# Moving one line of a hand-ordered kernel: WKV's transposes, a down product's place, and scales read as broadcasts

## The chip, the cores and the metric

The kernel runs on one core of one Trainium2 chip. The metric is the device time of one execution in microseconds (us). TensorE is called PE in the profile, VectorE DVE, ScalarE ACT, GpSimd POOL, SyncE SP; PEld is TensorE's loading of weights.

## The reference, cut to what matters

Four elements of 512 rows by 512 columns go through four residual steps each:

```python
x = x + tanh(g_xattn[0]) * wkv(w, u, layernorm(x), ctx)            # a scan over the rows
x = x + tanh(g_ffn[0])   * bitlinear_ffn(layernorm(x), w1, w2, w3)  # 512 -> 2048 -> 512
x = x + tanh(g_xattn[1]) * int8_attention(layernorm(x), ctx, ...)   # 16 heads
x = x + tanh(g_ffn[1])   * ternary_linear(x, gamma, W)              # 512 -> 512
```

WKV is a recurrence for each column with a running maximum. At each row it gives y = (A p + E v) / (A q + E); p, q and the maximum are carried on. The feed-forward quantises its inputs and hidden values in groups of 64 and has weights of one bit with one scale. The attention quantises rows and the weights of its query and output projections to 8 bits. The last step has ternary weights.

## The kernel before

An element's x stays in SBUF as four tiles of 128 rows. The four elements are staggered: while one is in its feed-forward, the element after it does WKV and the one before it does attention or the last step. The layers are generators, and each `yield` ends a step.

**The order of the work** is written by hand. A `line` is a generator with the places at which its steps come; `run` always takes the step with the smallest place. From the second element on, the unit of place is one element's feed-forward, divided into `SLOTS` = 17 parts. In this document a *place* is one such part: one unit of the feed-forward (one tile of rows by one quarter of the 2048 hidden columns). TensorE's instructions are pinned to this order, since the first of a step stands behind the last of the step before (`in_turn`, `next_turn`). Those of the other engines are placed by a scheduler that follows the dependencies and the program's order. Each engine then executes its instructions in order.

**The feed-forward** (`ffn_layer`) gives each unit four steps, at .0, .25, .5 and .75 of its place: the first up product with tanh (`gate`), the down product of the unit two back (`down`), the second up product with the gating and the quantising (`gated`), and the transposes of the unit before (`gate_parts`, tile tp_ps). The quantised hidden row goes through DVE (L736, maxima L231, reciprocal, product L666), ACT (L670) and POOL (L671). It is transposed, and is then split by ACT (L682) and DVE (L683) into the two parts of hr that the down product reads (ff_acc). The first element has its weights `made` beside it, in a first stage of its own that lasts to about 350 us.

**WKV** (`wkv_layer`) normalises and transposes the four row tiles (tiles wk_xn, one buffer; wk_ps; copy L573) and then treats four chunks of 128 columns. `in_steps(chains, 8)` starts a chunk every eight steps. A chunk's steps are: the maximum's scan (L588) and POOL's difference; two steps of relus and exponentials on ACT (L601, L603); the scan for q and the product with A; the scan for p (L623); the reciprocals (L629, two of 128x256); the product y (L634); the transposes of y (tile wy_ps) and the update of x (L640). A step is a quarter of a place, so a chunk takes two places. For elements 2 and 3 each chunk's v is loaded by a DMA of SP's queue into the one buffer that wk_xn also uses.

**The attention** of the element before has four steps a place, at .95, .20, .45 and .70: scores of one pair (s_ps, maximum L929, exponential L931), the values' product (o_ps) and transposes of the exponentials (pt_ps, copied by ACT L951), scores of the other pair, and again transposes and the collection of the output (ot_ps, at_o on DVE L989). Scores and up products share three PSUM banks (hp). All transposes, o_ps, ot_ps and query products share three others (m), so a transpose waits until the tile three before it in its ring has been read. In the first stage m has two banks.

**Scales.** Each row tile of attention is quantised with one scale a row. To have it along the columns, POOL fills a 128x128 tile with it (at_full, L848), and TensorE transposes that tile (sx_ps). Once, `output_scales` does the same for the output weights' scales: four copies on DVE (w_full, L429), four transposes (pb_ps), and one product (L431).

```python
def transpose(*args):
    return in_turn(nc.tensor.transpose(*args))
```

A transpose loads its input as weights and multiplies by the identity.

Of the kernel before, what the change touches and what calls it, by code (L numbers as in the profile page):

```python
# [10 lines left out]
F32 = mybir.dt.float32  # L11
# [5 lines left out]
ALU = mybir.AluOpType  # L17
# [4 lines left out]
P = 128  # L22
# [8 lines left out]
def kernel(  # L31
# [138 lines left out]
    def transpose(*args):  # L170
        return in_turn(nc.tensor.transpose(*args))  # L171
# [119 lines left out]
    class Weights:  # L291
# [132 lines left out]
        def output_scales(self):  # L424

            pb = bank("pb_ps")
            for j in range(NC):
                full = self.pool.tile([P, P], F32, name="w_full", tag="w_full", bufs=2)
                nc.vector.tensor_copy(full, self.sp[:, j : j + 1].to_broadcast([P, P]))  # L429
                transpose(pb[:, j * P : (j + 1) * P], full, ident)  # L430
            nc.vector.tensor_scalar(swp_b, pb, gates[:, 1:2], None, ALU.mult)  # L431
            nc.sync.dma_start(out=bp_b, in_=bcast(bp))
            nc.vector.tensor_scalar(bp_b, bp_b, gates[:, 1:2], None, ALU.mult)
# [117 lines left out]
    def wkv_layer(b, xb):  # L551

        kT = wk.tile([P, NC, T], F32, name=f"wk_k{b}", tag="wk_k")
        if b:
            r = layernorm(xb, pinned=True)
            yield  # L560
        else:
            r = layernorm(xb)
        for t in range(NT):
            if b or t == 0:
                xn = wk.tile([P, D], F32, name="wk_xn", tag="wk_v")
            else:
                xn = ff.tile([P, D], F32, name="wk_xn", tag="ff_a", bufs=3)
            centred(xn, xb, r, t)
            yield
            pt = bank("wk_ps")  # L570
            for c in range(NC):
                transpose(pt[:, c * P : (c + 1) * P], xn[:, c * P : (c + 1) * P], ident)
            nc.scalar.copy(kT[:, :, t * P : (t + 1) * P], blocks(pt))  # L573

        def chunk(c):
            def row(name):
                if b == 0 and c % 3:
                    return ff.tile([P, T + 1], F32, name=name, tag=(None, "ff_a", "xp")[c % 3], bufs=3)
                return wk.tile([P, T + 1], F32, name=name, tag=name)

            if b > 1:
                v = wk.tile([P, T], F32, name="wk_v", tag="wk_v")
                nc.sync.dma_start(out=v, in_=cD[b][:, c, :])
            k = kT[:, c, :]
            w_c, u_c, w_n, u_n = (a[:, c : c + 1] for a in (wc, uc, wcn, ucn))
            o = row("wk_o")
            nc.gpsimd.memset(o[:, 0:1], NEG_INF)
            nc.vector.tensor_tensor_scan(  # L588
                o[:, 1:], w_c.to_broadcast([P, T]), k, NEG_INF, ALU.add, ALU.max
            )  # L590

            if b == 0 and c < 3:
                e = ring.tile([P, 4, T], F32, name="wk_e", tag="w")
            else:
                e = wk.tile([P, 4, T], F32, name="wk_e", tag="wk_e")
            z = row("wk_p")[:, 0:T]
            nc.gpsimd.tensor_tensor(z, k, o[:, 0:T], ALU.subtract)
            if b:
                yield True
            for i, (sign, at) in enumerate(((1.0, u_c), (-1.0, w_c), (-1.0, u_n), (1.0, w_n))):  # L600
                nc.scalar.activation(e[:, i, :], z, AF.Relu, bias=at, scale=sign)  # L601
                if b and i % 2:
                    nc.scalar.activation(  # L603
                        e[:, i - 1 : i + 1, :], e[:, i - 1 : i + 1, :], AF.Exp, scale=-1.0
                    )
                    yield True
            if b == 0:
                exps[c] = nc.scalar.activation(e, e, AF.Exp, scale=-1.0)
                yield True

            A, E2, E, A2 = (e[:, i, :] for i in range(4))
            if b < 2:
                v = context.cT[b][:, c, :]
            q = row("wk_q")
            p = row("wk_p")
            nc.gpsimd.memset(q[:, 0:1], 0.0)
            nc.gpsimd.memset(p[:, 0:1], 0.0)  # L617
            nc.vector.tensor_tensor_scan(q[:, 1:], A2, E2, 0.0, ALU.mult, ALU.add)  # L618
            nc.gpsimd.tensor_tensor(E2, E2, v, ALU.mult)
            den = q[:, 0:T]  # L620
            nc.vector.tensor_tensor(den, A, den, ALU.mult)
            yield True
            nc.vector.tensor_tensor_scan(p[:, 1:], A2, E2, 0.0, ALU.mult, ALU.add)  # L623
            nc.gpsimd.tensor_tensor(den, den, E, ALU.add)
            nc.gpsimd.tensor_tensor(E, E, v, ALU.mult)
            yield True
            for h in range(2):
                half = den[:, h * (T // 2) : (h + 1) * (T // 2)]
                nc.vector.reciprocal(half, half)  # L629
            nc.gpsimd.tensor_tensor(A, A, p[:, 0:T], ALU.mult)  # L630
            nc.gpsimd.tensor_tensor(A, A, E, ALU.add)
            yield True
            y = E2
            nc.vector.tensor_tensor(y, A, den, ALU.mult)  # L634
            yield True
            pt = bank("wy_ps")
            for t in range(NT):
                transpose(pt[:, t * P : (t + 1) * P], y[:, t * P : (t + 1) * P], ident)
            xc = xb[:, :, c * P : (c + 1) * P]
            nc.vector.scalar_tensor_tensor(xc, blocks(pt), gates[:, 0:1], xc, ALU.mult, ALU.add)  # L640
            yield True

        chains = [chunk(c) for c in range(NC)]
        if b:
            yield from in_steps(chains, 8)
            return

        for chain in chains:
            next(chain)
            yield  # L650
        yield from in_steps(chains, (0, 1, 2, 4))
# [36 lines left out]
    def ffn_layer(xb, made=None):  # L688
# [88 lines left out]
            weights(1, 0)  # L777


        for n in range(len(units) + 2):  # L780
            now = n < len(units)
            if now:
                t, f = units[n]
                i = t % size


                if i == min(1, size - 1) and not made:
                    weights(2, f)
                after = units[n + 1] if n + 1 < len(units) else None
                if after and after[1] != f and not made:  # L790
                    weights(0, after[1])
                z = gate(up(t, f, 0))
            yield
            if n > 1:
                down(*units[n - 2])
            yield
            if size == NT and n + 1 < NT:
                inputs_parts(n + 1)
                next_turn()
            if now:  # L800
                gated(t, f, z, up(t, f, 1))
            if now and after and after[1] != f and not made:
                weights(1, after[1])
            yield
            if 0 < n <= len(units):
                gate_parts(*units[n - 1])

            if now and size < NT:
                next_turn()
                if (t, f) in ((0, 1), (1, 2)):  # L810
                    inputs(f + 1)
                elif (t, f) in ((1, 1), (1, 3)):
                    inputs_parts(2 if f == 1 else 3)
            if n < len(units) + 1:
                yield
# [4 lines left out]
    def attention_layer(b, xb, pool, tiles=range(NT)):  # L820
# [18 lines left out]
        def prepared(t, r):  # L839
            xn = row("at_xn")  # L840
            centred_aside(xn, xb, r, t)
            s = sm.tile([P, 2], F32, name="at_s", tag="at_s")
            yield True
            absmax(s[:, 0:1], xn)
            int8_scale(s[:, 0:1], s[:, 1:2], s[:, 0:1])
            rounded(xn, s[:, 1:2])
            full = row("at_full")[:, 0:P]
            nc.gpsimd.tensor_scalar(full, ones, s[:, 0:1], None, ALU.mult)  # L848
            yield True
            transposed_rows(xqT[:, :, t * P : (t + 1) * P], xn)  # L850
            sp = bank("sx_ps")[:, 0:P]
            transpose(sp, full, ident)
            nc.scalar.copy(sxb[:, t * P : (t + 1) * P], sp)

            nc.gpsimd.tensor_tensor(xb[:, t, :], xb[:, t, :], bp_b, ALU.add)
            yield True
# [312 lines left out]
    with (  # L1169
# [105 lines left out]
        for b in (2, 3):  # L1275
            line(
                next_batch(b),
                (b - 1.0 - 4.2 / SLOTS, b - 1.0 - 4.2 / SLOTS, 1),
                (b - 1.0 - 3.2 / SLOTS, b - 1.0 - 3.2 / SLOTS, 1),
                (b - 1.0 + 1.8 / SLOTS, b - 1.0 + 5.8 / SLOTS, 4),  # L1280
                (b - 1.0 + 5.05 / SLOTS, b - 1.0 + 13.05 / SLOTS, 32),
            )
        run(0.99)
    nc.sync.dma_start(out=gamma_b, in_=bcast(gamma))
# [75 lines left out]
```

## Time and profile before

| what | value |
|---|---|
| time, median of 3 runs | 1141.91 us (1141.67 to 1142.8) |
| the profiled execution's own time | 1140.58 us |
| its span | 1138.8 us |
| mean granted TensorE clock | 0.948 |
| PE busy | 967.2 us (85%), 5520 instructions |
| DVE busy | 877.1 us (77%), 1889 |
| ACT busy | 722.0 us (63%), 1482 |
| POOL busy | 320.4 us (28%), 317 |

The profile is of one execution. A row of the timeline has a start, a duration, the engine, the line, the operation, output<-inputs and, in brackets, how long the engine had been idle before it and what ended that. Where an instruction waits for several others, the one that came last is named. Rows can merge neighbours (x2, x8). A row of the table by stretch has, for each engine, the busy time and the number of instructions, and then the granted clock, the DMA engines' share and their rate.

### The profile page before, as it was taken

What the parts mean: (1) busy time and instruction counts of PE and PEld (TensorE: products, weight loads), DVE (VectorE), ACT (ScalarE), POOL (GpSimd) and SP (SyncE); (2) the same over time, 40 slices, a digit from 0 to 9 for tenths busy, and PEclk for the clock granted to TensorE, in tenths of its full rate; (3) what the DMA queues carried; (4) which work ended last, traced back from release to release, by engine and by line L of the source; (5) the groups of instructions that cost most, each with busy time, mean ns of one, the idle gap of its engine ahead of it and who ended that gap; (6) DMA issues with size and microseconds to landing.
All of it is one profiled execution on the core that took longest, in us unless ns stands there. A gap on an engine that the chain in (4) does not pass through costs nothing.

```text
span 1138.8 us, 16572 instructions
## 1 busy us (share of the span) xinstructions
PE 967.2 (85%) x5520; PEld 679.9 (60%) x5548; DVE 877.1 (77%) x1889; ACT 722.0 (63%) x1482; POOL 320.4 (28%) x317
## 2 busy tenths in 40 slices
PE   4887898888877968889998897999999899888983
PEld 3344565555555756666776565777777677555651
DVE  5965547679878788999769899977689756688766
ACT  5777555454214576757777677687676577877763
POOL 3821014341305244441124535412122410112000
PEclk8898999999889989999998999999999999998997
DMA  8197745364425545654645544565474572333400
GB/s 277 47 299 281 282 163 184 116 236 148 148 76 192 209 166 177 186 164 169 226 173 185 169 162 137 174 217 163 176 234 149 181 232 76 105 109 103 126 5 37
DMA packets 85668, 189.58 MB, mean 166 GB/s; under 512 B 12240, under 2 KB 36816, under 8 KB 74576
## 3 DMA queue, kind: packets, MB, share of 16 engines
q1 hardware_dynamic: 85584, 188.53, 49.4%
q8 instruction: 44, 0.72, 0.3%
q14 instruction: 40, 0.33, 0.1%
HBM read 148.65 MB, written 39.85 MB: 166 GB/s over the span
## 4 chain that ended last, share of the span: by engine, by line
PE 47%; DVE 27%; ACT 15%; issue 4%; POOL 4%; DMA 2%; SPq 0%; ACTq 0%; POOLq 0%; DVEq 0%
PE ff_hp L168 13%; PE ff_acc L168 7%; PE pt_ps L171 6%; PE o_ps L168 4%; PE s_ps L168 3%; PE v_ps L168 3%; ACT at_P L931 3%; DVE at_nm L929 3%; DVE wk_q L629 3%; DVE qg_i L666 2%; PE qr_ps L171 2%; ACT wk_e L601 2%; PE tp_ps L171 2%; DVE wk_q L618 2%; ACT at_PT L951 2%
## 5 line engine op out<-in xcount | busy, mean ns | idle before, releaser
L168 PE MATMUL ff_hp<-wT,xp 128*128 128x512 f32 x1024 | 275.8, 413 | 5.9 <-ACT at_P L931 2.1
L168 PEld LDWEIGHTS ff_hp<-wT,xp 128*128 128x128 f32 x1024 | 197.0, 196 | 56.4 <-ACT at_P L931 4.6
L931 ACT ACTIVATE at_P<-s_ps,at_nm 128x512 f32<-128x512 f32 x256 | 174.6, 689 | 72.3 <-DVE at_nm L929 71.0
L929 DVE TENSOR_REDUCE at_nm<-s_ps 128x1 f32<-128x512 f32 x256 | 165.8, 678 | 28.5 <-PE s_ps L168 28.3
L671 POOL TENSOR_TENSOR ff_z<-qg_b,qg_s 128x512 f32<-128x512 bf16 x64 | 72.5, 1132 | 335.3 <-ACT qg_b L670 293.0
L951 ACT COPY at_PT<-pt_ps 128x512 f32<-128x512 f32 x224 | 124.0, 596 | 38.5 <-PE pt_ps L171 38.0
L171 PE MATMUL pt_ps<-ident,at_P 128*128 128x128 f32 x1024 | 140.9, 279 | 8.0 <-ACT at_PT L951 2.6
L168 PE MATMUL ff_acc<-wT,hr 128*128 128x512 f32 x512 | 137.9, 411 | 6.1 <-ACT hr L682 3.4
L171 PEld LDWEIGHTS pt_ps<-ident,at_P 128*128 128x128 f32 x1024 | 113.8, 141 | 48.9 <-issue 14.1
L168 PEld LDWEIGHTS ff_acc<-wT,hr 128*128 128x128 f32 x512 | 93.5, 192 | 27.0 <-ACT hr L682 4.3
L168 PE MATMUL s_ps<-at_kR,at_qR 128*128 128x512 f32 x256 | 97.6, 452 | 13.2 <-ACT at_P L931 5.4
L670 ACT CAST qg_b<-qg_i 128x512 bf16<-128x512 int8 x80 | 49.3, 617 | 59.8 <-DVE qg_i L666 53.8
L168 PE MATMUL o_ps<-at_PT,at_V 128*32 128x256 f32 x1024 | 73.0, 399 | 1.8 <-ACT at_PT L951 1.2
L731 ACT ACTIVATE ff_z<-ff_hp,coef 128x512 f32<-128x512 f32 x64 | 43.8, 684 | 46.4 <-PE ff_hp L168 42.9
L736 DVE SCALAR_TENSOR_TENSOR ff_z<-ff_hp,coef,ff_z 128x512 f32<-128x512 f32 x64 | 47.5, 743 | 29.4 <-PE ff_hp L168 29.1
L732 DVE SCALAR_TENSOR_TENSOR ff_z<-ff_z,ff_hp 128x512 f32<-128x512 f32 x64 | 43.6, 681 | 32.7 <-ACT ff_z L731 32.3
L168 PE MATMUL v_ps<-wkvT,cT 128*128 128x512 f32 x128 | 63.2, 642 | 4.2 <-ACT wT L316 3.2
L168 PE MATMUL k_ps<-cT,wkvT 128*128 128x512 f32 x128 | 61.1, 626 | 2.3 <-ACT wk_k L573 1.0
L168 PEld LDWEIGHTS s_ps<-at_kR,at_qR 128*128 128x128 f32 x256 | 45.5, 196 | 28.3 <-ACT at_P L931 13.1
L682 ACT CAST hr<-tp_ps 128x512 fp32r<-128x512 f32 x64 | 37.6, 587 | 35.6 <-PE tp_ps L171 35.6
L629 DVE RECIPROCAL wk_q<-wk_q 128x256 f32<-128x256 f32 x32 | 54.3, 1719 | 1.4 <-POOL wk_p L617 1.4
L171 PE MATMUL tp_ps<-ident,ff_z 128*128 128x128 f32 x256 | 39.9, 279 | 18.1 <-ACT at_PT L951 7.7
(179 smaller groups left out, 1757.3 us busy)
## 6 DMA issues: line engine op xcount, KB each, us to landing
wT<-wD SPq DMA_DIRECT2D x72, 1024.0 KB, 5.2
wn<-in_L_ffn_w_dram SPq DMA_DIRECT2D x18, 1024.0 KB, 6.2
at_kR<-kD SPq DMA_DIRECT2D x128, 128.0 KB, 2.9
at_qR<-qD SPq DMA_DIRECT2D x256, 64.0 KB, 2.2
wD<-wT SPq DMA_DIRECT2D x12, 1024.0 KB, 4.5
kD<-k_half SPq DMA_DIRECT2D x16, 512.0 KB, 3.2
qD<-at_half SPq DMA_DIRECT2D x32, 256.0 KB, 2.0
cn<-in_ctx_dram SPq DMA_DIRECT2D x8, 512.0 KB, 6.2
```

Source lines behind the costliest of these rows:

```text
L168: return in_turn(nc.tensor.matmul(*args, **kwargs))
L171: return in_turn(nc.tensor.transpose(*args))
L629: nc.vector.reciprocal(half, half)
L670: nc.scalar.copy(qb, qi)
L671: nc.gpsimd.tensor_tensor(grouped(src), grouped(qb), s.unsqueeze(2).to_broadcast([P, NG, GS]), ALU.mult)
L682: nc.scalar.copy(part[:, 0, :], pt)
L731: nc.scalar.activation(z, hp, AF.Tanh, scale=coef[:, 0:1])
L732: nc.vector.scalar_tensor_tensor(z, z, 1.0, hp, ALU.add, ALU.mult)
L736: nc.vector.scalar_tensor_tensor(z, hp, coef[:, 1:2], z, ALU.mult, ALU.mult)
L929: nc.vector.tensor_reduce(nm, sp, AX.X, ALU.max, negate=True)
L931: nc.scalar.activation(lanes[k, i, t], sp, AF.Exp, bias=nm, accum_out=sums[k][:, t, i : i + 1],)
L951: made[k] = nc.scalar.copy(dst, blocks(pt))
```

## The change

Four things. (1) In WKV for elements 1 to 3 an empty step stands between y and its transposes, so these come two steps after y; they now share a step with the beginning of the next chunk, which goes first in the program. The line of elements 2 and 3 has its 32 steps at 4.40 to 12.40 places instead of 5.05 to 13.05 (0.65 sooner), and its four normalising steps begin at 1.40 instead of 1.80. A chunk needs one more step, and the last transposes fall on the line's end. (2) In the first element's feed-forward the down product comes after the second up product, not before it. (3) The output scales are transposed from the column, repeated by a broadcast, without a copy. (4) So are the attention's row scales, without POOL's fill; the row buffer that it took is free for others.

```diff
             for j in range(NC):
-                full = self.pool.tile([P, P], F32, name="w_full", tag="w_full", bufs=2)
-                nc.vector.tensor_copy(full, self.sp[:, j : j + 1].to_broadcast([P, P]))
-                transpose(pb[:, j * P : (j + 1) * P], full, ident)
+                transpose(
+                    pb[:, j * P : (j + 1) * P],
+                    self.sp[:, j : j + 1].to_broadcast([P, P]),
+                    ident,
+                )
...
             nc.vector.tensor_tensor(y, A, den, ALU.mult)
             yield True
+            if b:
+                yield True
             pt = bank("wy_ps")
...
             yield
-            if n > 1:
-                down(*units[n - 2])
-            yield
+            if not made:
+                if n > 1:
+                    down(*units[n - 2])
+                yield
...
+            if made:
+                yield
+                if n > 1:
+                    down(*units[n - 2])
             yield
             if 0 < n <= len(units):
                 gate_parts(*units[n - 1])
...
-            full = row("at_full")[:, 0:P]
-            nc.gpsimd.tensor_scalar(full, ones, s[:, 0:1], None, ALU.mult)
             yield True
             transposed_rows(xqT[:, :, t * P : (t + 1) * P], xn)
             sp = bank("sx_ps")[:, 0:P]
-            transpose(sp, full, ident)
+            transpose(sp, s[:, 0:1].to_broadcast([P, P]), ident)
...
-                (b - 1.0 + 1.8 / SLOTS, b - 1.0 + 5.8 / SLOTS, 4),
-                (b - 1.0 + 5.05 / SLOTS, b - 1.0 + 13.05 / SLOTS, 32),
+                (b - 1.0 + 1.40 / SLOTS, b - 1.0 + 5.40 / SLOTS, 4),
+                (b - 1.0 + 4.40 / SLOTS, b - 1.0 + 12.40 / SLOTS, 32),
```

## The prediction

> **What bounds the kernel now.** I read the page's busy shares first, then its chain, then the table by stretch, then the timeline around the edited lines.
>
> ```profile
> PE 967.2 (85%) x5520; PEld 679.9 (60%) x5548; DVE 877.1 (77%) x1889; ACT 722.0 (63%) x1482; POOL 320.4 (28%) x317
> ...
> PE 47%; DVE 27%; ACT 15%; issue 4%; POOL 4%; DMA 2%; SPq 0%; ACTq 0%; POOLq 0%; DVEq 0%
> ```
>
> No engine is full over the span, and the chain goes back and forth between PE and DVE. So the stages matter. From one WKV transpose group to the next, in the stage where element 2's WKV runs (three of its four chunks):
>
> ```profile
> core 0: us, PE busy (x) PEld busy (x) DVE busy (x) ACT busy (x) POOL busy (x), PEclk, DMA share, GB/s
> 417.80:445.90 28.10, 24.55 (x144) 18.89 (x145) 23.33 (x37) 18.72 (x39) 10.92 (x12) 0.90 0.50 164
> 445.90:473.10 27.20, 24.24 (x143) 17.85 (x144) 25.22 (x40) 18.82 (x39) 11.36 (x12) 0.94 0.49 168
> 473.10:499.30 26.20, 22.12 (x141) 16.63 (x141) 25.44 (x50) 17.94 (x39) 13.55 (x14) 0.99 0.57 177
> ```
>
> A chunk's period is two places of the order, 27.2 us on average. DVE works 24.7 of it (97% in the last row), PE 22 to 24.5. Inside one period:
>
> ```profile
> 467.29 3.33 DVE L629 RECIPROCAL wk_q<-wk_q 128x256 f32<-128x256 f32 x2
> ...
> 469.90 0.63 PE L171 MATMUL tp_ps<-ident,ff_z 128*128 128x128 f32 x4
> ...
> 470.55 1.21 DVE L929 TENSOR_REDUCE at_nm<-s_ps 128x1 f32<-128x512 f32 x2
> ...
> 471.68 0.73 DVE L736 SCALAR_TENSOR_TENSOR ff_z<-ff_hp,coef,ff_z 128x512 f32<-128x512 f32 x1
> ...
> 472.34 0.67 DVE L634 TENSOR_TENSOR wk_e<-wk_e,wk_q 128x512 f32<-128x512 f32 x1
> ...
> 473.16 0.63 PE L171 MATMUL wy_ps<-ident,wk_e 128*128 128x128 f32 x4 [2.63 <-ACT hr L682]
> ```
>
> PE stops at 470.53 for WKV's transposes and starts 0.15 us after the product y (L634) ends. The row names the cast hr, but the other long stops (at 417.83, 445.93, 499.29, 691.42) also begin 0.14 or 0.15 us after their y, so y is what they wait for. Y is late because the two reciprocals (3.33 us) stand ahead of the maxima and of L736. These stops are 4.08 + 3.13 + 2.63 + 3.00 = 12.8 us for element 2 and 2.91 us for element 3, where three of four groups find y ready.
>
> **What the skill says.** "Perfetto Trace Analysis", section Identifying the Most-Contended Engine: occupancy is a fair measure for Vector, but matmul busy time is not for Tensor. The table agrees: 97% of DVE is a floor, 84 to 89% of PE is not. "SBUF — State Buffer", section SBUF: two separate sides: an instruction of VectorE with two SBUF inputs and one of GpSimd that reads SBUF shut each other out. The trace fits: the quantising multiply L666 took 1.33 us at 461.43, with POOL at work, and 0.68 us at 475.13. "TensorE: Matmul & The Clock Gate", section LDWEIGHTS: a load goes by its columns, about 128/1.2 = 107 ns; the trace has 138 to 141 ns. It says nothing of a column repeated 128 times, and no row shows one.
>
> **Part 1, the WKV line.** It runs for elements 1 (inside the first stage), 2 and 3. For 2 and 3 the chunk steps begin at 4.40 instead of 5.05 places; y moves from .55 to .90 of a place, and its transposes from .80 to the next place's .40, two quarter-places after y instead of one: some 6.8 us of order instead of 3.4, against stops of at most 4.1. They should then find y ready. What is late next: the reciprocals move from just ahead of the second scores' maxima to behind the second up's quantising. From the end of that up, DVE needs 0.73 (L736) + 0.67 + 0.33 + 0.68 + 3.33 = 5.7 us to the reciprocals' end, then 0.27 for at_o and 0.68 for hr's second half, 6.7 us. These two free the banks for the next at_P transposes. PE meanwhile has 1.04 + 0.56 + 0.63 + 0.70 + 2.05 + 1.07 = 6.05 us. So a wait of some 0.2 us stays, or 0.9 where L666 meets POOL. The floor is DVE: no DVE work of WKV disappears. At the third row's 97% a period is 24.7/0.97 = 25.4 us, 1.8 less than now. I take 1.5 times four: **−6** (from 0, if the waits only move, to −12.8). For element 3 the three periods between 628.8 and 723.6 have DVE busy for 86.9 of 94.8 us; 95% would be 91.5. With one stop there I take **−2** (+3 to −5).
>
> A cost: the fourth norm step (4.40) and the first chunk step (4.40) now meet, where a score pair and an up lay between. The row tile has one buffer, so transposes of tile 3 must follow transposes of tile 2, a copy and the norm:
>
> ```profile
> 389.22 0.60 PE L171 MATMUL wk_ps<-ident,wk_xn 128*128 128x128 f32 x4
> ...
> 389.90 0.59 ACT L573 COPY wk_k<-wk_ps 128x512 f32<-128x512 f32 x1
> ...
> 390.38 0.83 ACT L224 ACTIVATE wk_xn<-xb,ln_r 128x512 f32<-128x512 f32 x1
> ```
>
> PE's order is fixed, so it stands from 389.82 to about 391.3: 1.5 us, for two elements **+3** (+2.5 to +5, if ACT is held by the query halves). The second up and everything behind it wait.
>
> The other instructions of the line move too: per chunk three scans, two products, the reciprocals and the update of x on DVE, six ACT rows, POOL's products, and SP's load of v. SP is passed by nothing that needs it soon: v still comes four steps after its buffer's last reader, and queries behind it are fetched two places ahead. Element 1 gets the later transposes alone; its stops were 0.67 + 0.56 us: 0 (−1 to +1).
>
> **Part 2, the first element's down product.** The down moves behind the second up. The same matmuls run; the quantised hidden row gets one more down (2.1 us) before its transposes, the tanh one less before L736 wants it. At the end of this feed-forward:
>
> ```profile
> 345.45 0.65 PE L171 MATMUL tp_ps<-ident,ff_z 128*128 128x128 f32 x4 [2.05 <-POOL ff_z L671]
> ...
> 347.19 0.49 PE L168 MATMUL ff_acc<-wT,hr 128*128 128x512 f32 x1 [1.08 <-ACT hr L682]
> ```
>
> The last second up comes 2.1 us sooner in PE's order, so the 2.05 us goes: **−2** (−3 to 0); the 1.08 stays, as cast and down remain neighbours. In the body most stops are for copies out of two banks: 0 (−3 to +3).
>
> **Part 3, the scales.** Four copies of 0.22 us leave DVE. They stood behind the ternary rounding:
>
> ```profile
> 325.25 0.47 PE L171 MATMUL pb_ps<-ident,w_full 128*128 128x128 f32 x1 [4.44 <-DVE w_full L429]
> ...
> 326.88 0.74 DVE L431 TENSOR_SCALAR swp_b<-pb_ps,gates 128x512 f32<-128x512 f32 x1
> ...
> 327.67 0.59 PE L171 MATMUL wt_ps<-identb,wi 128*128 128x128 bf16 x4 [0.37 <-DVE swp_b L431]
> ```
>
> PE no longer stops at 320.8, but 1.1 us of transposes later it wants the bank that L431 frees, on the same DVE queue. L431 can come some 1.3 us sooner (four copies' 0.88 and its place): **−1.3** (0 to −4.4). Sixteen POOL fills of 0.60 us go; the few PE waits for them sum to 1 us, so **−0.4** (−1 to 0). Twenty weight loads read one repeated column; at twice 0.14 us they cost 2.8 us more, at best nothing changes; loads mostly overlap: 0.
>
> Sum: −6 − 2 + 3 − 2 − 1.3 − 0.4 = **−8.7 us**. The profiled execution took 1140.58 us (span 1138.8 and 1.8 around it), so 1131.9; its like in the median's terms is 1.3 higher, 1133.2.
>
> **Rivals.**
> *The whole stop is won.* 15.7 us of stops go, the clock (0.90 and 0.94 in two rows) comes up, 4.4 at the scales: −15.7 − 4.4 − 2 + 3 = −19, 1123 us. For it: PE would fit. Against: DVE has only 7.5 us idle (4.77 + 1.98 + 0.76) in the three periods.
> *The wait only moves.* DVE stays at its pace, the stop appears before the scores or at_P transposes: +3 − 2 − 1.3 = 0, 1142 us. For it: in the row above, the scores' exponentials end at about 472.5 and the next scores want those banks, so removing y alone would win under 1 us; it is the reciprocals' new place that must do the rest. That the change does nothing at all (the stop being hr's) gives the same.
> *Slower: the reciprocals hold the banks.* If DVE is 2 us behind PE when they begin, at_o and hr end near 8.7 us against PE's 6.05, a 2.6 us stop in each of eight periods, 21 us, for 15.7 removed; with +3 and −3.3 elsewhere 1147 us. It decides from 1.8 us of lag on. For it: DVE is 91 to 97% busy. Against: now they delay maxima, exponentials and y in one go, and at_o and hr have 6.05 us of PE work to hide behind where y had 1.83 (468.70 to 470.53).
>
> **Numbers.** Forecast 0.60 (1127 to 1139), whole stop 0.12, wait moves 0.14, slower 0.14. A difference of 0.2%, 2.3 us, is about what a measurement tells from none. Faster: 0.60 + 0.12 + 0.04 of the third = 0.76; same 0.08; slower 0.14 + 0.02 = 0.16. The likeliest is 1133.2; leaving a tenth on either side, 1125 to 1143.
>
> **What would show it.** Right: WKV's transposes without stops of 2 us, periods near 25.5 us with DVE at 96%, a new stop of 1.5 us at wk_ps for elements 2 and 3, nothing at pb_ps but a stop at wt_ps, none at the last tp_ps. Wrong: pt_ps waiting over 2 us for at_o or hr behind L629, longer periods, or the first stage longer by over 3 us because L736 waits for tanh.

## The result, and the profile after

The change made the kernel slower: 1153.63 us median (1149.25 to 1156.23) against 1142.36 us for the kernel before on the same chip, a ratio of 1.008 with a 95% interval of 1.0059 to 1.0101. The forecast was 1133.2. The profiled execution after took 1153.5 us, its span is 1151.7; before it was 1140.58 and 1138.8. The 1140.58 lies under that kernel's medians, and of the 12.9 us between the two profiles some 4 are not the change's: by the ratio it costs 9. Every profile here is of an undisturbed execution but e11's, which ran at a clock of 0.822 and for which no stage lengths are given.

Line numbers move: the first up's tanh L731 is now L736 (ACT), its product, here **the gate**, L732 is L737, the second up's product L736 is L741; WKV's scan q L618 is L620, E·v L619 is L621, scan p L623 is L625, the reciprocals L629 are L631.

The page after, busy shares and chain:

```profile
PE 976.1 (85%) x5520; PEld 690.2 (60%) x5548; DVE 876.1 (76%) x1885; ACT 722.3 (63%) x1482; POOL 307.5 (27%) x301
...
PE 50%; DVE 22%; ACT 11%; POOL 6%; issue 6%; DMA 4%; SPq 1%; ACTq 0%; POOLq 0%; DVEq 0%
```

The same number of matmuls takes 8.9 us longer, at a lower granted clock (0.948 before, 0.934 after), and DVE is as busy as it was. POOL's share of the chain went from 4 to 6%. Which stage lost? Cut where the last residual update of each feed-forward starts, both spans give:

| stage | before | after | difference |
|---|---|---|---|
| element 0's feed-forward (weights made beside it) | 351.1 | 344.8 | −6.3 |
| element 1's feed-forward, element 2's WKV | 201.4 | 207.5 | +6.1 |
| element 2's feed-forward, element 3's WKV | 222.7 | 231.7 | +9.0 |
| element 3's feed-forward | 188.9 | 189.7 | +0.8 |
| the rest | 174.7 | 178.0 | +3.3 |

Each length is of one execution. In the thirteen kernels here whose first stage is the same program (after's), that stage lies between 341.7 and 346.6 us, so differences of 1 or 2 us are not read. The 3.3 us of the rest are PE's busy time (133.2 to 137.4), not new stops. The first stage won what was forecast and more. The loss lies in the two stages in which the WKV line was moved, first before and then after:

```profile
351.10:552.50 201.40, 173.07 (x1007) 130.87 (x1011) 171.67 (x350) 133.02 (x274) 73.13 (x74) 0.96 0.56 185
552.50:775.20 222.70, 199.99 (x1229) 150.23 (x1236) 188.99 (x405) 158.59 (x331) 83.39 (x78) 0.96 0.52 175
...
344.80:552.30 207.50, 178.54 (x1006) 135.17 (x1010) 171.08 (x354) 133.72 (x274) 70.70 (x68) 0.93 0.52 174
552.30:784.00 231.70, 200.38 (x1229) 152.50 (x1237) 190.87 (x405) 158.66 (x331) 79.13 (x74) 0.94 0.52 171
```

Of the 15.1 us lost, 5.9 is PE's busy time (slower matmuls) and 9.2 its idle time. The two stages differ in this: element 2's has 5.5 us more of busy time and only 0.6 more of idle time, element 3's 0.4 and 8.6.

The table by stretch after, again from one WKV transpose group of element 2 to the next:

```profile
408.60:438.60 30.00, 25.17 (x137) 19.10 (x138) 25.80 (x40) 19.43 (x40) 12.08 (x13) 0.83 0.62 215
438.60:468.80 30.20, 25.33 (x147) 19.34 (x146) 25.08 (x38) 18.70 (x40) 12.25 (x12) 0.89 0.30 94
468.80:497.00 28.20, 23.94 (x144) 18.32 (x144) 25.23 (x52) 18.66 (x41) 9.56 (x10) 0.94 0.69 236
```

A period is 2 to 3 us longer than before (28.10, 27.20, 26.20). DVE has about as much to do (2.5 us more in the first row), so it is now idle for 3 to 5 us of each. The clock is lower in all three rows.

The stops that the prediction named, in the timeline after:

```profile
321.84 0.59 PE L171 MATMUL wt_ps<-identb,wi 128*128 128x128 bf16 x4 [5.08 <-DVE swp_b L433]
...
340.30 1.06 PE L171 MATMUL tp_ps<-ident,ff_z 128*128 128x128 f32 x4
...
383.34 0.66 PE L171 MATMUL wk_ps<-ident,wk_xn 128*128 128x128 f32 x4 [1.39 <-ACT wk_xn L224]
...
408.58 0.63 PE L171 MATMUL wy_ps<-ident,wk_e 128*128 128x128 f32 x4 [1.32 <-DVE wk_e L636]
```

The 4.44 us at pb_ps went, and 5.08 us at the next reader of swp_b took its place. The last tp_ps has no stop. The back-to-back norms stop PE for 1.39 us, and for 1.39 again in element 3. Of the 15.7 us at WKV's transposes 2.0 is left, 1.32 here and 0.68 for element 3. All of that is as forecast. What was not forecast is the first row of PE's waits after (waited for, us in total, times, longest):

```profile
PE ff_hp L168 <- DVE ff_z L737: 21.3, 6, 8.1
```

In the kernel before, this wait (for L732) comes to 0.2 us. One of the six, with DVE and POOL:

```profile
448.76 2.02 DVE L620 TENSOR_TENSOR_SCAN wk_q<-wk_e 128x512 f32<-128x512 f32 x1
449.16 0.68 ACT L736 ACTIVATE ff_z<-ff_hp,coef 128x512 f32<-128x512 f32 x1
450.89 0.69 DVE L623 TENSOR_TENSOR wk_q<-wk_e,wk_q 128x512 f32<-128x512 f32 x1
450.92 1.78 POOL L621 TENSOR_TENSOR wk_e<-wk_e,wk_v 128x512 f32<-128x512 f32 x1 [1.22 <-PE ff_acc L168]
...
452.74 2.27 DVE L625 TENSOR_TENSOR_SCAN wk_p<-wk_e 128x512 f32<-128x512 f32 x1 [1.15 <-POOL wk_e L621]
...
454.93 0.66 DVE L737 SCALAR_TENSOR_TENSOR ff_z<-ff_z,ff_hp 128x512 f32<-128x512 f32 x1
...
455.64 3.78 PE L168 MATMUL ff_hp<-wT,xp 128*128 128x512 f32 x8 [4.34 <-DVE ff_z L737]
```

The tanh ends at 449.84, and the gate could follow. But on DVE's queue scan q, the product and scan p stand ahead of it. Scan p needs E·v, which overwrites what scan q reads, so POOL starts it only when scan q ends (POOL's row names a matmul that ends at about the same time). The chain q, E·v, p takes until 455.0. Then the gate reads its bank, and only then may the second up write to it. In the kernel before, the same chunk has the gate ahead of scan p:

```profile
457.51 1.22 DVE L618 TENSOR_TENSOR_SCAN wk_q<-wk_e 128x512 f32<-128x512 f32 x1
...
465.56 0.67 DVE L732 SCALAR_TENSOR_TENSOR ff_z<-ff_z,ff_hp 128x512 f32<-128x512 f32 x1
466.16 1.21 DVE L623 TENSOR_TENSOR_SCAN wk_p<-wk_e 128x512 f32<-128x512 f32 x1
```

DVE's order of the eight chunks of elements 2 and 3, read for scans, products, gates, maxima and reciprocals alone, has "q, product, p, gate" with nothing between in four chunks after and in none before. Those four have the stops of 3.21, 4.34, 3.48 and 8.14 us. (In two chunks before, scan p comes ahead of a gate too, with maxima or reciprocals between, and the second up has no stop over 1 us there.) In element 2's stage the new stops took the place of the old ones: PE's waits at wy_ps fell from 12.8 to 1.3 us there, and those at ff_hp rose from 2.0 to 11.0.

### The profile page after: what moved, and what is told of

Same layout as the page of the kernel before. It is cut to its first block, busy times and chain, and to the rows that moved or that the text cites. A ratio compares the mean times of both kernels' runs of the same rounds, so it can differ in the third digit from the quotient of the medians.

```text
span 1151.7 us, 16550 instructions
## 1 busy us (share of the span) xinstructions
PE 976.1 (85%) x5520; PEld 690.2 (60%) x5548; DVE 876.1 (76%) x1885; ACT 722.3 (63%) x1482; POOL 307.5 (27%) x301
## 4 chain that ended last, share of the span: by engine, by line
PE 50%; DVE 22%; ACT 11%; POOL 6%; issue 6%; DMA 4%; SPq 1%; ACTq 0%; POOLq 0%; DVEq 0%
PE ff_hp L168 15%; PE pt_ps L171 7%; PE ff_acc L168 6%; PE o_ps L168 4%; PE s_ps L168 3%; PE v_ps L168 3%; ACT at_P L940 3%; PE tp_ps L171 2%; DVE at_nm L938 2%; DVE wk_q L631 2%; PE qr_ps L171 2%; ACT at_PT L960 2%; PE ot_ps L168 1%; PE f_ps L168 1%; DVE qg_i L671 1%
## 5 line engine op out<-in xcount | busy, mean ns | idle before, releaser
L168 PE MATMUL ff_hp<-wT,xp 128*128 128x512 f32 x1024 | 282.2, 421 | 25.0 <-DVE ff_z L737 21.3
L168 PEld LDWEIGHTS ff_hp<-wT,xp 128*128 128x128 f32 x1024 | 201.0, 201 | 77.4 <-DVE ff_z L737 24.1
L676 POOL TENSOR_TENSOR ff_z<-qg_b,qg_s 128x512 f32<-128x512 bf16 x64 | 69.8, 1091 | 380.3 <-ACT qg_b L675 327.6
L171 PE MATMUL pt_ps<-ident,at_P 128*128 128x128 f32 x1024 | 145.4, 285 | 10.3 <-ACT at_PT L960 2.6
L171 PEld LDWEIGHTS pt_ps<-ident,at_P 128*128 128x128 f32 x1024 | 117.9, 145 | 52.6 <-issue 15.9
L736 ACT ACTIVATE ff_z<-ff_hp,coef 128x512 f32<-128x512 f32 x64 | 43.8, 685 | 65.6 <-PE ff_hp L168 59.3
L741 DVE SCALAR_TENSOR_TENSOR ff_z<-ff_hp,coef,ff_z 128x512 f32<-128x512 f32 x64 | 47.4, 741 | 33.1 <-PE ff_hp L168 32.9
L737 DVE SCALAR_TENSOR_TENSOR ff_z<-ff_z,ff_hp 128x512 f32<-128x512 f32 x64 | 43.3, 677 | 18.7 <-ACT ff_z L736 18.4
L631 DVE RECIPROCAL wk_q<-wk_q 128x256 f32<-128x256 f32 x32 | 54.9, 1729 | 3.1 <-POOL wk_q L626 1.6
```

The costliest lines, as they stand in the source:

```text
L168: return in_turn(nc.tensor.matmul(*args, **kwargs))
L676: nc.gpsimd.tensor_tensor(grouped(src), grouped(qb), s.unsqueeze(2).to_broadcast([P, NG, GS]), ALU.mult)
L736: nc.scalar.activation(z, hp, AF.Tanh, scale=coef[:, 0:1])
L737: nc.vector.scalar_tensor_tensor(z, z, 1.0, hp, ALU.add, ALU.mult)
L741: nc.vector.scalar_tensor_tensor(z, hp, coef[:, 1:2], z, ALU.mult, ALU.mult)
```

## The experiments

**Theory.** The new places let DVE's order put scan p, and its wait for POOL, ahead of the gate; the up's bank is freed late. **Rivals.** The empty step or the other parts do it; the place against the attention, not the order, does it; DVE is full, and any order gives this.

### The parts apart

e1 is the kernel after with the old places; e2 is the kernel before with the new places alone; e3 and e4 are the kernel before with one other part each.

```diff
e1 (from after)
-  (b - 1.0 + 1.40 / SLOTS, ..., 4), (b - 1.0 + 4.40 / SLOTS, ..., 32)
+  (b - 1.0 + 1.80 / SLOTS, ..., 4), (b - 1.0 + 5.05 / SLOTS, ..., 32)
e2 (from before)
-  (b - 1.0 + 1.80 / SLOTS, ..., 4), (b - 1.0 + 5.05 / SLOTS, ..., 32)
+  (b - 1.0 + 1.40 / SLOTS, ..., 4), (b - 1.0 + 4.40 / SLOTS, ..., 32)
e3 (from before): only the down product behind the second up where made
e4 (from before): only the scales transposed from broadcast columns
```

> The changed kernel with WKV's old places (1.8 and 5.05); the empty step, the down order and the broadcasts stay. Theory (the phase within a place: at 4.40 the scans for q and p stand ahead of the gate's L737 on VectorE, and the second up waits): no up product waits over 1.5 us for the gate in elements 2 and 3, the first stage is still some 6 us shorter, so 1133 to 1139 us. Rival (the empty step costs: the update of x gets between the scores' maxima): about 1154 us, as the changed kernel.

> The kernel before with WKV's new places (1.40 and 4.40) alone. Theory (phase): the waits of ff_hp for the gate, 21 us in six stops in the changed kernel, are here too, and no gain of the first stage: 1153 to 1162 us. Rival (the empty step or the down order costs): about 1142 us.

> The kernel before with the first element's down products behind the second up, alone. The first stage was 6.3 us shorter in the changed kernel. If the down order does it: 1136 to 1139 us. If the broadcasts do it: within 2 us of the kernel before.

> The kernel before with the broadcast scales alone. If only the wait moves from pb_ps to wt_ps, as in the changed kernel's profile (5.1 us at wt_ps for swp_b): within 1.5 us of the kernel before. If the broadcasts are what shortens the first stage: 1136 to 1139 us.

| kernel | us, median (range) | ratio to before, same chip | WKV stage of element 2, 3 |
|---|---|---|---|
| e1 | 1133.07 (1131.48 to 1137.32) | 0.9912 [0.9881, 0.9943] | 200.9, 221.7 |
| e2 | 1154.92 (1153.85 to 1157.89) | 1.0100 [1.0066, 1.0134] | 201.7, 234.9 |
| e3 | 1138.78 (1135.58 to 1142.55) | 0.9944 [0.9915, 0.9974] | 202.9, 222.1 |
| e4 | 1141.70 (1138.35 to 1147.67) | 0.9969 [0.9957, 0.9982] | 201.4, 222.2 |

Whether the whole gains or loses hangs on the places. Everything else together is a gain of 0.9%. The down order shortens the first stage by 5.0 us (351.1 to 346.1), the broadcasts by 0.8; by their ratios, e3 and e4 as a whole gain some 6.4 and 3.5 us. The empty step, whose work is WKV's stages, goes with 0.5 and 1.0 us less there, no more than stages vary. Its wait moved. PE's waits in e1 (the same row for the kernel before: 5.4 us, 11 times, longest 1.2):

```profile
PE s_ps L168 <- ACT at_P L940: 13.9, 18, 2.2
```

y's stops of 15.7 us went, and the next scores wait 8.5 us more for their banks. e2 has just one long ff_hp stop (3.28 us), where its expectation had six. Its loss is in element 3's stage alone, with stops at wy_ps and tp_ps (5.16, 5.53, 7.52 us). Element 2's stage is as long as before (201.7 against 201.4); its first transposes of y still wait 4.12 us, as before (4.08). So the new places are bad without the empty step too, but not by the same waits, and element 2 loses only where they meet the other parts (207.5), of which the empty step is the one in its WKV.

### Place or phase

A chunk step at 4.40 differs from one at 5.05 in its place and in its phase, .40 or .05 of a place, against the ups at .0 and .5.

```diff
e5 (from after)
+  0.80 and 4.05 in place of 1.40 and 4.40
e6 (from after)
+  2.40 and 5.40 in place of 1.40 and 4.40
```

> The changed kernel with WKV at 0.80 and 4.05: a whole place sooner than before, with the old phase within a place. Theory (phase): 1133 to 1140 us, no long wait of ff_hp for the gate. Rival (sooner is what costs, since WKV then meets more of the attention two elements back): slower than the changed kernel, 1155 us or more.

> The changed kernel with WKV at 2.40 and 5.40: a place later, with the new phase. Theory (phase): again slow, 1150 to 1160 us, with waits of ff_hp for the gate of 3 us and more. Rival (sooner is what costs): 1142 us or less.

e5 took 1135.33 us (0.992 [0.9889, 0.9951]), in its range; its stages are 198.7 and 226.9. But where no long ff_hp stop was expected, element 2's stage has three, of 2.12, 3.41 and 2.02 us, and is shorter than before all the same. A late gate is not enough to make a stage longer. e6 took 1136.5 (0.9947 [0.9928, 0.9966]), a miss: the same phase one place later costs little (202.7, 225.5). In e6 scan p stands ahead of the gate in two chunks, not four, and its stops for the gate are 3.63, 2.78 and 2.70 us. The phase alone is not the cause; the order that comes out of it is a better candidate.

### The order on DVE

e9 pins scan p behind the newest gate; e10 leaves the order free, but takes E·v from POOL, so that scan p waits for no other engine.

```diff
e9 (from after)
-            nc.vector.tensor_tensor_scan(p[:, 1:], A2, E2, 0.0, ALU.mult, ALU.add)
+            scan = nc.vector.tensor_tensor_scan(p[:, 1:], A2, E2, 0.0, ALU.mult, ALU.add)
+            if b > 1:
+                behind(scan, gates_done[0])      # gates_done[0]: the latest unit's gate
e10 (from after)
-            nc.gpsimd.tensor_tensor(E2, E2, v, ALU.mult)
+            (nc.vector if b > 1 else nc.gpsimd).tensor_tensor(E2, E2, v, ALU.mult)
```

> The changed kernel with one more dependency: in elements 2 and 3 the scan for p stands behind the latest gate's L737 on VectorE. Theory (in the changed kernel four chunks have scan q, product, scan p and only then L737, and scan p waits for POOL's product of E and v; the second up waits for the bank that L737 frees): the four stops of ff_hp of 3.2 to 8.1 us fall under 1.5 us, and with them part of the halved clock; 1138 to 1146 us. Rival of the prediction (the reciprocals hold the banks): no change, 1150 us or more, since the reciprocals stay where they are.

> The changed kernel with the product of E and v on VectorE in elements 2 and 3 (eight instructions of about 0.7 us move from POOL to DVE). Theory (L737 is held behind a scan for p that waits 1.2 us for POOL and then runs at 2.3 us instead of 1.2 to 1.5): the scan no longer waits, ff_hp stops less, 1138 to 1148 us, though VectorE has 5.6 us more to do. Rival (VectorE's sum is the only bound): 1158 us or more.

e9 took 1143.0 us (0.9975 [0.9961, 0.9989]), e10 1141.98 (0.9946 [0.9918, 0.9974]). Each takes back 1.0 to 1.3% of before, which is more than element 2's stage: of the 11.0 us between the spans of after and e9, 4.9 are in that stage and 5.8 in the rest, where nothing was changed. The same spot in e9's timeline:

```profile
448.70 0.68 DVE L740 SCALAR_TENSOR_TENSOR ff_z<-ff_z,ff_hp 128x512 f32<-128x512 f32 x1
...
449.44 2.12 PE L168 MATMUL ff_hp<-wT,xp 128*128 128x512 f32 x8 [0.92 <-DVE ff_z L740]
...
449.94 2.30 DVE L626 TENSOR_TENSOR_SCAN wk_p<-wk_e 128x512 f32<-128x512 f32 x1 [0.56 <-POOL wk_e L622]
```

The gate runs while POOL makes E·v, and the stop of 4.34 us is 0.92. Element 2's stage is 202.6 in e9 and 197.9 in e10, against 207.5: most of its loss was this order. The two runs don't separate the order from the wait for POOL, since in e10 the scheduler itself put the gate ahead of scan p in all eight chunks. But element 3's stage hardly moves (232.3 and 231.5, against 231.7). Of the four stops, all expected under 1.5 us, e9 still has two there, of 1.58 and 5.37 us. In e10 the gate stops ff_hp for no more than 2.6 us at a time in this stage, and other waits are as long (PE's waits in 542.8 to 774.3):

```profile
PE s_ps L168 <- ACT at_P L940: 4.9, 4, 3.5
PE qr_ps L171 <- ACT tf_xn L246: 4.3, 1, 4.3
PE ff_hp L168 <- DVE ff_z L737: 3.7, 2, 2.6
```

So the order of scan p and gate alone doesn't explain element 3.

### Element 3

e11 is the kernel after with element 3 alone at its old places. e12 is e9, with the ternary step's row maxima behind the gate too. e13 is e9 with the norms at 1.00, so that the last doesn't meet the first chunk.

```diff
e11 (from after)
+  element 2: 1.40, 4.40; element 3: 1.80, 5.05
e12 (from e9), in the ternary step
+        if not last:
+            behind(top, gates_done[0])      # top: the row maxima
e13 (from e9)
-  (b - 1.0 + 1.40 / SLOTS, ..., 4)
+  (b - 1.0 + 1.00 / SLOTS, ..., 4)
```

> The changed kernel with the old places (1.80, 5.05) for element 3's WKV alone; element 2 keeps the new ones. In the changed kernel element 2's stage is 6.2 us longer and element 3's 8.9 us. Theory (each element's loss comes from its own WKV places): about 9 us faster than the changed kernel, 1143 to 1147 us, with element 2's two long ff_hp stops still there. Rival (element 2's late WKV pushes what follows): under 4 us faster.

> e9_gate_before_scan with, besides, the row maxima of the last step (which wait on VectorE for POOL's tf_xn) behind the latest gate's L737. e9 mended element 2's stage but left element 3's at 232 us against 223. Theory (in element 3's stage other instructions that wait for POOL stand ahead of L737 too; at 707 us ff_hp still stopped 5.4 us): element 3's stage at 224 to 229 us, 3 to 8 us under e9. Rival (the loss of element 3 is the start, places 4 to 6, where the attention of two elements still runs): no change from e9.

> e9_gate_before_scan with the four norm steps at 1.00 to 4.00 instead of 1.40 to 4.40, so that the fourth no longer meets the first chunk step at 4.40. The two stops of PE at wk_ps of 1.39 us should go: 2 to 4 us under e9. If something else waits in their place: within 1 us of e9.

e11 took 1140.23 us (0.9923 [0.9897, 0.9949]), some 1.6% under after, and so more than the 9 us that were expected of its stage. On its DVE queue scan p still stands right ahead of the gate in two of element 2's chunks, and in none of element 3's. e12 took 1155.89 (1.0077 [1.0053, 1.0100]): a miss. With the maxima pinned, the stop of 5.37 us at ff_hp is 7.63, a new one of 3.88 stands at the ternary transposes, and element 3's stage went to 239.6. e13 took 1140.37 (0.9941 [0.9917, 0.9964]); its wk_ps stops are gone and element 3's stage is 228.3, 4.0 under e9's.

The next two move one of element 3's two parts, with element 2 at its old places.

```diff
e16 (from after)
+  element 2: 1.80, 5.05; element 3: norms 1.40, chunks 5.05
e19 (from after)
+  element 2: 1.80, 5.05; element 3: norms 1.00, chunks 4.40
```

> Kernel after with element 2's line at its old places (1.80, 5.05) and element 3's normalising steps at 1.40 but its chunk steps at the old 5.05. Theory A (the chunk steps' places carry element 3's loss, through DVE's order and the long stops in its last two chunks, with the lower clock after them): element 3's WKV stage 222 to 224 us and 1132 to 1137 in all, as with both lines old (1133.1). Theory B (the normalising steps carry it, since they come earlier against the attention two elements back and bunch with the first chunk): stage 227 or more, 1139 or more.

> Kernel after with element 2's line at its old places, element 3's chunk steps at the new 4.40 and its normalising steps at 1.00, so that they stand apart from the first chunk. DVE's order has scan q, product, scan p, gate in element 3's chunks 3 and 4, as in the kernel after. Theory A: stage 227 to 233 us, two stops at ff_hp of 3 and 5 to 8 us, clock under 0.96 in the stage, 1138 to 1144. Theory B: stage 222 to 225, 1132 to 1137.

e16 took 1131.22 us (0.9875 [0.9836, 0.9913]), e19 1140.74 (0.9955 [0.9940, 0.9969]). Element 3's stage in e16 and then in e19, from the table by stretch:

```profile
541.60:762.70 221.10, 197.69 (x1237) 148.56 (x1237) 191.59 (x405) 158.04 (x331) 80.64 (x74) 0.98 0.55 177
```

```profile
542.50:771.60 229.10, 197.37 (x1237) 149.75 (x1236) 190.53 (x406) 158.12 (x331) 79.22 (x74) 0.96 0.52 170
```

The chunks' places cost 8.0 us, all of it PE's idle time, and the norms' earlier place nothing by itself. (e19's norms stand at 1.00, not 1.40, so that none meets the first chunk.) The longest stop of e19, in its last chunk:

```profile
691.82 0.69 DVE L231 TENSOR_REDUCE tf_s<-tf_xn 128x1 f32<-128x512 f32 x1 [1.45 <-POOL wk_p L619]
...
692.88 2.17 DVE L620 TENSOR_TENSOR_SCAN wk_q<-wk_e 128x512 f32<-128x512 f32 x1
...
693.76 0.67 ACT L736 ACTIVATE ff_z<-ff_hp,coef 128x512 f32<-128x512 f32 x1
...
695.12 1.77 POOL L621 TENSOR_TENSOR wk_e<-wk_e,wk_v 128x512 f32<-128x512 f32 x1 [1.16 <-DVE tf_s L1117]
...
696.92 2.27 DVE L625 TENSOR_TENSOR_SCAN wk_p<-wk_e 128x512 f32<-128x512 f32 x1 [1.16 <-POOL wk_e L621]
...
699.69 0.67 DVE L737 SCALAR_TENSOR_TENSOR ff_z<-ff_z,ff_hp 128x512 f32<-128x512 f32 x1
...
700.42 3.78 PE L168 MATMUL ff_hp<-wT,xp 128*128 128x512 f32 x8 [8.21 <-DVE ff_z L737]
```

It is the same chain with one more link ahead: the ternary maxima wait for POOL's product with gamma (it ends at 691.79; the row names a memset behind it), so scan q begins late, runs slowly beside POOL, and scan p with its wait comes before the gate. (Of the 8.21 us, 2.2 lie before the tanh's end at 694.43.) At the old places the last chunk's scans come two thirds of a place later, and PE has no ff_hp stop over 1.5 us in e16's stage.

### Do the parts add, and is there a better version?

```diff
e17 (from e9)
+  element 2: 1.40, 4.40; element 3: 1.80, 5.05
e18 (from after)
+  element 2: 1.40, 4.40; element 3: 1.80, 5.05
-            nc.gpsimd.tensor_tensor(E2, E2, v, ALU.mult)
+            (nc.vector if b == 2 else nc.gpsimd).tensor_tensor(E2, E2, v, ALU.mult)
```

> Kernel after with scan p pinned behind the gate's last product for elements 2 and 3, and element 3's line at its old places. If element 2's loss is the order of scan p and gate and element 3's is its places, the two gains add: element 2's stage 202 to 204, element 3's 222 to 224, 1131 to 1136 (0.988 to 0.992 of before). If they are one and the same, no better than element 3's old places alone: 0.992 or more.

> Kernel after with element 2 at its new places and its product E v on VectorE, and element 3 at its old places with E v on GpSimd. The best stage lengths seen put together: element 2's 198 (as with E v on VectorE for both), element 3's 222, so 3 us under the kernel with both lines old: 1129 to 1132, 0.987 to 0.990 of before. If a stage's length hangs on how the one before it ends, element 3's goes to 225 or more and nothing is won: 1133 or more.

e17 took 1139.03 us (0.9950 [0.9930, 0.9970]), a miss: not better than e11. Element 2's stage is 202.6, as expected, but element 3's is 227.0. The pin holds there as well, where the order was good already: in two of element 3's chunks it pushes scan p from ahead of the reciprocals to behind them and a gate. So the pin is no cure at every place, and the gains don't add.

e18 took 1128.22 us (0.9857 [0.9816, 0.9897]). Element 2's stage is 196.3, the shortest of all, element 3's 224.6. It beats the kernels before and after; from e16 (0.9875) it isn't told apart.

### Is DVE the floor?

e14 is e1 without the reciprocals of elements 2 and 3. It leaves the division out.

```diff
e14 (from e1)
-            for h in range(2):
+            for h in range(2 if b < 2 else 0):
```

> e1_old_places (all of the change but the new places) without the reciprocals of elements 2 and 3: leaves out 8 pairs of 3.33 us on VectorE, 27 us, so y is A times the denominator there. Theory of the prediction (VectorE's sum is the floor of a chunk's period): periods fall from 27 us to about 24.5 and the time by 14 to 22 us, to 1111 to 1119. Rival (not the sum, but round trips between PE, VectorE and ACT bound a period): less than 8 us faster than e1.

It took 1138.06 us (0.9909 [0.9877, 0.9942]), against 0.9912 for e1: nothing won. DVE's busy time in the two stages fell from 172.63 to 164.07 and from 191.61 to 181.01 us, while the stages went from 200.9 to 202.3 and from 221.7 to 229.1. PE's waits in e14 show two that e1 has not, or has smaller (tp_ps 5.8 in e1):

```profile
PE tp_ps L171 <- ACT at_PT L960: 17.6, 11, 5.3
...
PE ff_hp L168 <- DVE ff_z L741: 7.5, 4, 4.2
```

With less work the scheduler arrives at another order, and other round trips wait. So DVE's sum is not what bounds these stages. The waits point to round trips between PE, ACT, DVE and POOL in a fixed order; that is argued from them, not tried by a run.

## Why the prediction was wrong

**Part 1, what is late next: the step that failed.** It took y's later transposes as the main effect and named the reciprocals, before at_o and hr, as the next thing late. Only the part of the queue from the reciprocals on was worked through. The scans move too, and the text counted them among what moves without asking what they would stand in front of. In four of eight chunks scan p with its wait for POOL came ahead of the gate, and PE stopped for the second up's bank, 3.2 to 8.1 us each time. With half of the +3 for the norms in each, the forecast was −4.5 us for element 2's stage and −0.5 for element 3's; they came out at +6.1 and +9.0.

For element 2, e9 and e10 show the order as the cause of most of it. Its new stops only replaced the old ones, and the stage lost by its clock (0.964 before, 0.934 after, 0.958 in e9), for which the forecast has no term. For element 3, e16 and e19 show the chunks' places as the cause, 8.0 us. How they act stays open: the same chain stands in its last chunk, but e10 has the gate first and the stage is no shorter.

The wait of 0.2 us that the text took from 6.7 against 6.05 us doesn't follow from these two, which differ by 0.65. Nothing hangs on it, since the longest wait of pt_ps for at_o or hr after the change is 0.28 us.

**The floor.** "24.7/0.97 = 25.4" took DVE's sum for a bound that the change could approach. It pointed to a gain where none was: e14 took work from DVE and won nothing. The reading of the Trainium skill behind it ("Perfetto Trace Analysis", Identifying the Most-Contended Engine) was too strong: a high occupancy was there, and was not the limit.

**The removed stops.** That y is what the transposes waited for was right, as 13.7 of 15.7 us went. What it was worth was not: e1 has y's stops removed at the old places and its WKV stages are 1.5 us shorter, which one execution each can't tell from none. The second rival, that the wait only moves to the scores' banks, was right for the empty step and had its place named; it was given 0.14.

**The slower rival** had the right sign (1147 us; measured 1153.63) and the wrong mechanism: pt_ps does not wait for at_o or hr behind the reciprocals. It looked at work behind the reciprocals, when the new stops came from the scans ahead of the gate.

**The norms' cost**, +3, measured: two stops of 1.39, 2.8 us. e13 without them was 4.0 us shorter in element 3's stage, and 0.6 us longer in element 2's.

**Part 2**, −2, was mis-sized: −5.0 for the first stage in e3. The 2.05 us at the last tp_ps is gone as forecast; the other 3 us lie in the body, at the edge of the range given, and no run here says where. A first stage varies by up to 5 us between kernels that share it, so the size is rough.

**Part 3**, −1.3 − 0.4, measured −0.8 in e4's first stage and −3.5 by e4's ratio. The stop at wt_ps came as named. The broadcast columns cost nothing in the median, 137 ns against 140, though one load took 230: the groups of sx_ps's weight loads before and then after (min/median/max ns):

```profile
L171 PEld LDWEIGHTS sx_ps<-ident,at_full x16: 138/140/143, 356.4 to 982.6; 128*128 128x128 f32 x16
```

```profile
L171 PEld LDWEIGHTS sx_ps<-ident,at_s x16: 132/137/230, 352.5 to 992.2; 128*128 128x128 f32 x16
```

## What to carry to other kernels

When a line of work is moved against others in a fixed order, list every instruction of it that waits for another engine, and ask for each what stands behind it on its queue at the new place, above all the reader that frees a bank for PE. A stop that is removed is worth only what the next wait leaves of it; one run with the stop removed and nothing moved tells that. Compare idle time and busy time stage by stage before a new stop is blamed: it may only have replaced an old one. A busy share of 97% in a stage full of round trips is no floor until a run with less work on that engine is faster.

## What the runs showed of the hardware

A scan of 128x512 takes 1.2 us by itself, and up to 2.3 beside a product of POOL. Which of the two is slowed goes by the start. In the timeline after, POOL first, and then the scan first:

```profile
424.42 1.26 POOL L626 TENSOR_TENSOR wk_q<-wk_q,wk_e 128x512 f32<-128x512 f32 x1
424.49 2.27 DVE L625 TENSOR_TENSOR_SCAN wk_p<-wk_e 128x512 f32<-128x512 f32 x1 [1.18 <-POOL wk_e L621]
...
614.19 1.22 DVE L625 TENSOR_TENSOR_SCAN wk_p<-wk_e 128x512 f32<-128x512 f32 x1
...
614.41 2.06 POOL L626 TENSOR_TENSOR wk_q<-wk_q,wk_e 128x512 f32<-128x512 f32 x1 [1.99 <-DVE wk_q L623]
```

The later one takes longer by about the rest of the earlier one. That agrees with the Trainium skill ("SBUF — State Buffer", section SBUF: two separate sides): of an instruction of VectorE with two SBUF inputs and one of GpSimd that reads SBUF, whichever starts first has the shared ports for its whole length, and the other waits. In the queue ahead of the gate this adds a microsecond to scan p, beside the wait for E·v.

A long stop of PE also goes with a lower clock. The table by stretch after, around the 8.14 us stop that ends at 712.30 (the clock is the third number from the end):

```profile
702.00:712.00 10.00, 2.15 (x10) 1.41 (x8) 7.41 (x16) 3.81 (x8) 8.59 (x8) 0.74 0.84 269
712.00:717.00 5.00, 4.70 (x14) 3.83 (x15) 3.98 (x6) 1.48 (x5) 2.64 (x3) 0.50 0.00 0
717.00:722.00 5.00, 4.17 (x29) 3.11 (x29) 4.39 (x10) 2.97 (x5) 0.00 (x0) 1.00 0.02 5
```

The first matmuls after the stop run at half the clock for some 5 us: in the table they have 0.50, and the next stretch 1.00. e19's stretch behind its 8.21 us stop has 0.57. The Trainium skill ("TensorE: Matmul & The Clock Gate", section Part 1: The HAM clock gate) has half the clock after an idle window of about 3.4 us, and full clock after as long a busy one; these two stops agree with it. But no wholly idle window is needed. In element 2's stage of e1 no stop is longer than 2.17 us, and there are half-clock stretches all the same:

```profile
407.80:411.20 3.40, 1.23 (x6) 0.69 (x5) 3.40 (x5) 2.38 (x6) 3.32 (x3) 1.00 0.63 162
411.20:414.60 3.40, 3.40 (x11) 2.62 (x10) 3.40 (x8) 0.21 (x1) 0.40 (x3) 0.50 0.03 7
```

PE was busy for 1.23 of 3.40 us, and the next 3.40 us had half the clock. So of the price of stops a part, here 5.9 of 15.1 us, is not idle time, and the forecast's sum of stops leaves it out. Why after's stops cost element 2 more clock than before's, for about the same idle time, no run here shows.
